# A graph layer whose source rows GpSimd gathers: SyncE also fetches one unit in 72 row by row, and rows, own rows and sets of edges are asked for sooner

## The chip, the cores and the metric

The kernel runs on one core of a Trainium2 chip. The metric is the device time of one execution in microseconds (us); three runs of the kernel before took 15,397.0, 15,399.93 and 15,401.84 us, so the median is 15,399.93 us. A profile of one further execution is read beside it. Engines are named as the profile does: PE is TensorE, DVE is VectorE, ACT is ScalarE, POOL is GpSimd, SP is SyncE (SPq and ACTq are their queues of transfers).

## What is computed

One layer of an equivariant graph network with 50,000 nodes of 160 numbers and 1,650,000 edges, sorted by target. Each edge takes the row of its source node, multiplies it with its own four numbers and with small weight matrices, and the results are summed at the target node; then come a second matrix, a residual and a normalisation.

```
ss, vv = (s[src], v[src])                      # 1,650,000 rows of 160 floats, by index
...
m = jnp.concatenate([out0, out1.reshape(-1, 3 * MUL1)], axis=1)
m_agg = jax.ops.segment_sum(m, dst, num_segments=n)
...
return x + jax.nn.relu(h)                      # h: m_agg times Ws and Wv
...
x = _layernorm(x + _L0_gnn_ref(x, edge_attr_4, ...), axis=-1)
```

The last 50,000 edges of the input are loops of a node to itself; sorted in, each node has one. The kernel takes such an edge out of the list that it gathers for, except at the start, and adds the node's own row in another way.

## The kernel before

**Units, tiles, sets.** 128 edges are a *unit*: one gather, one matmul. Six units (`G`) are a group, three groups (`PG`) a *tile*: 18 units; the program calls a tile a pair. There are 12,516 units in 696 tiles. Seven tiles, 126 units, are a *set of edges* (`SG` = 21 groups); there are 100. The weights are folded into one matrix that is applied after the sums, so per unit only the sums remain: the 128 gathered rows (`xg`, 128 × 160) are multiplied with a 128 × 128 operand `ha`, which holds for each edge its four numbers at the column of its target within a window of 32 nodes.

**The engines' parts.** GpSimd gathers: for each unit an indirect transfer (L433) takes 128 rows of `x` by the offsets in `sources`, into one of four tiles `xg`. VectorE lays out each set (`place`, L358 on: offsets for the gathers at L315, relative targets `rel`, the edges' numbers `pk`), builds `ha` for a tile (`spread`: L442, L445) `AHEAD` = 3 tiles ahead, and turns a tile's sums out of PSUM and adds them to a ring of nodes in SBUF (`turn_sums`: L488, L497). TensorE multiplies (L474), and for finished nodes applies the weights (`block`, L812). The order of SyncE, TensorE, VectorE and ScalarE is the order in which the program is written; GpSimd is arranged by the framework.

**Units that ScalarE fetches.** Every 2.5 tiles from tile 21 on, one unit (the last of its tile) is not gathered. `ask_alone` (L402) reads its 128 addresses from a tile `where` into ScalarE's registers, 32 at a time (L416), and issues 128 plain transfers of one row of 640 bytes each (L421), three after each gather of the loop, from `LEAD` = 4 tiles ahead. They land in one of three tiles `alone_scalar`. TensorE waits for a semaphore that all 128 transfers of the unit raise before it multiplies them. `address` (L394) makes `where` from a set's sources.

**What SyncE does.** All other transfers, in the order of the program: a set's edges (`load`, L259: `raw`, and `fd` with the first target of each group), asked at the first tile of the set before; the nodes' rows for the residual (`xt`, L741) and the results (`out`, L906), in blocks of four times 128 nodes, so about every seven tiles; and the nodes' own rows (`xr`, `sa`: L773, L776), asked five tiles before their part of the ring begins. The write of `out` waits until VectorE has normalised the rows.

**Packs.** The loops are taken out by packing: 128 rows of 790 edges are read (L571 to L575), VectorE finds the loops, moves the later edges up by masked copies (L600 to L663), and SyncE writes each row to its place in the list `edges`, and the loops' numbers to `selves` (`store`, `put`: L698, L715). A pack is a list of 57 steps, the last 17 of which store, 8 rows and 16 transfers each; there are 16 packs. The steps are spread evenly over the time up to the pack's due tile (L973), by which the first set that reads those edges, or the first own rows, need it.

```
for step in packs[0][done:todo]:
    if step:
        step()
```

**How long cover lasts.** `xg` has four tiles, so GpSimd may run three tiles beyond the one that TensorE works on; `sums` of three tiles fit in PSUM.

Of the kernel before, what the change touches and what calls it, by code (L numbers as in the profile page):

```python
# [39 lines left out]
F32 = mybir.dt.float32  # L40
# [10 lines left out]
P = 128  # L51
# [16 lines left out]
PG = 3  # L68
# [9 lines left out]
KM = 31  # L78
AHEAD = 3
SUMS = 3  # L80

ALONE = {"scalar": (2.5, 0, 3)}
LEAD = 4
SEMS = 16
AT_ONCE = 32

# [25 lines left out]
def tile_gnn_resnorm(ctx: ExitStack, tc: tile.TileContext, x, src, dst, attr, W1, W2, W3, W4, W5, Ws, Wv, out, n_edges):  # L112
# [120 lines left out]
    with tc.tile_pool(name="once", bufs=1) as once, tc.tile_pool(name="raw", bufs=2) as rawp, \  # L233
# [7 lines left out]

        wherep, alonep = (later_pools.enter_context(tc.tile_pool(name=name, bufs=bufs))
                          for name, bufs in (("where", 2), ("alone", 3)))
        spotp, ownp = (later_pools.enter_context(tc.tile_pool(name=name, bufs=bufs))
# [148 lines left out]

        def address(s, at, fd, ef, af):  # L394

            where = wherep.tile([P, NK, W], I32, name="where")
            clipped = where.bitcast(F32)
            nc.vector.tensor_scalar(clipped, ef[:, 0], 0.0, float(N - 1), op0=ALU.max, op1=ALU.min)
            nc.vector.tensor_scalar(where, clipped, 4.0 * D, None, op0=ALU.mult)
            where_of[s] = where, at[0]  # L400

        def ask_alone(name, p):  # L402
# [5 lines left out]
            eng, kind = {"sync": (nc.sync, ET.SP), "scalar": (nc.scalar, ET.Activation)}[name]  # L408
            to = alonep.tile([P, D], F32, name=f"alone_{name}")
            sem, uses = kept[name][asked[name] % SEMS], asked[name] // SEMS + 1  # L410
# [452 lines left out]
        def after_pair(p, f, *args):  # L863
            later.setdefault(p, []).append((f, args))
# [43 lines left out]
        def do_cast(s):  # L908
            raws[s] = cast(raws[s])
            address(*raws[s])  # L910

# [83 lines left out]

        to_ask = {name: deque(range_of(every, at)) for name, (every, at, _) in ALONE.items()}
        asking = {}
        turning = None
        for p, (s, g, ng) in enumerate(pairs):
            if p % per == 0 and s + 1 < NSC:  # L1000
                end = reach(s + 1)
                assert end <= 0 or rows_stored[0] == NR or end <= row_start(rows_stored[0])[0][0]
                raws[s + 1] = load(s + 1)
                if s + 2 == NSC:
                    after_pair(p + 4, examine_all)
                    after_pair(p + 6, read_flags)
            if p % per == 2 and s + 1 < NSC:
                do_cast(s + 1)
            rows = gather(s, placed[s], (g - s * SG) * G, ng * G, {b: came[p, b][0] for b in (1, 2) if (p, b) in came})
            for j, ps in enumerate(group_sums(p, rows, has.pop(p))):  # L1010
# [200 lines left out]
```

## Time and profile before

| | |
|---|---|
| median of three runs | 15,399.93 us |
| the profiled execution's own time | 15,395.35 us |
| its span in the profile | 15,393.3 us |
| GpSimd busy | 11,614.3 us (75%) |
| TensorE busy | 10,745.6 us (70%) |
| VectorE busy | 6,891.3 us (45%) |
| ScalarE busy (without issuing transfers) | 138.6 us (1%) |
| TensorE's granted clock | 0.576 |
| moved by the transfer engines | 1,347.79 MB, mean 88 GB/s |

Issuing of transfers by SyncE and ScalarE is not counted as busy; for GpSimd's gathers the issuing itself is the instruction, and it is counted. In a row of groups stand the line, the engine, the operation, output and inputs, the count, then the busy time and the mean in ns of one, then the idle time just before them and what ended most of it. In a row of waits stand who waited for whom, the total in us, how many times, and the longest. The idle time of an engine is of no cost where another engine sets the time.

### The profile page before, as it was taken

How to read it: one execution, taken by the hardware profiler on the slowest of the kernel's cores; microseconds unless marked ns; L12 is line 12 of the kernel's file. 1: busy time of each engine (PE TensorE's matmuls, PEld its weight loads, DVE VectorE, ACT ScalarE, POOL GpSimd, SP SyncE). 2: the span in 40 equal slices, each digit the busy share in tenths (PEclk: the TensorE clock that was granted, in tenths of full speed). 3: DMA queues.
4: the chain of work that ended last, by engine and by line, in shares of the span. 5: the costliest groups of instructions: out<-in, count | busy, mean ns of one | idle time of the engine just before them, and what ended most of it. 6: DMA issues, size and time to landing. Idle time of an engine off the chain costs nothing.

```text
span 15393.3 us, 164322 instructions
## 1 busy us (share of the span) xinstructions
PE 10745.6 (70%) x28959; PEld 6884.0 (45%) x28960; DVE 6891.3 (45%) x9468; ACT 138.6 (1%) x172; POOL 11614.3 (75%) x12263
## 2 busy tenths in 40 slices
PE   6767767676667676666766776766767676667666
PEld 3444444444444444444444444444444444444444
DVE  5534535344353544535344453544535435354333
ACT  0000000000000000000000000000000000000000
POOL 7777777777777777777777777777777777777777
PEclk5555555555555555555556555555555555555555
DMA  3333333333333333333333333333333333333332
GB/s 99 81 99 80 86 93 82 97 83 89 90 85 91 86 87 90 86 92 83 96 84 85 95 80 98 80 88 90 84 95 82 90 90 84 92 85 85 84 83 71
DMA packets 778898, 1347.79 MB, mean 88 GB/s; under 512 B 277566, under 2 KB 536537, under 8 KB 761621
## 3 DMA queue, kind: packets, MB, share of 16 engines
q0 software_dynamic: 587952, 1004.22, 27.7%
q1 hardware_dynamic: 120272, 310.14, 7.3%
q10 hardware_dynamic: 69616, 22.89, 0.8%
q14 instruction: 828, 6.77, 0.2%
q8 instruction: 230, 3.77, 0.1%
HBM read 1264.17 MB, written 72.09 MB: 87 GB/s over the span
## 4 chain that ended last, share of the span: by engine, by line
POOL 60%; issue 23%; DMA 12%; PE 4%; DVE 1%; POOLq 0%
POOL xg L433 60%; DMA xg<-in_x,sources 12%; PE ps L474 3%; PE phb L812 0%; DVE ha L445 0%; DVE xt L815 0%; DVE st L817 0%; DVE xr L791 0%; DVE ring L497 0%; DVE prow L663 0%; DVE ring L795 0%; DVE pri L658 0%; DVE sums L488 0%; DVE mv L819 0%; DVE marks L656 0%
## 5 line engine op out<-in xcount | busy, mean ns | idle before, releaser
L433 POOL DMA_INDIRECT xg<-in_x,sources x12249 | 11609.0, 948 | 3753.2 <-issue 3539.1
L474 PE MATMUL ps<-xg,ha 128*128 128x160 f32 x24498 | 9834.9, 513 | 4624.8 <-DMA xg<-in_x,sources 4521.5
L474 PEld LDWEIGHTS ps<-xg,ha 128*128 128x128 f32 x24498 | 5780.7, 293 | 8482.6 <-DMA xg<-in_x,sources 8005.4
L488 DVE STREAM_TRANSPOSE sums<-ps 128x480 f32<-128x480 f32 x696 | 474.3, 681 | 6929.9 <-PE ps L474 6909.2
L445 DVE TENSOR_TENSOR ha<-hot,pk 128x2304 f32<-128x2304 f32 x696 | 1776.0, 2552 | 23.9
L812 PE MATMUL phb<-BWk,ring 128*128 128x160 f32 (+1 forms) x3910 | 1294.8, 421 | 6.0 <-issue 5.2
L812 PEld LDWEIGHTS phb<-BWk,ring 128*128 128x128 f32 (+1 forms) x3910 | 1104.5, 325 | 7.0 <-issue 5.5
L497 DVE TENSOR_TENSOR ring<-ring,sums 128x160 f32 x2086 | 684.6, 328 | 354.2 <-issue 206.8
L815 DVE SCALAR_TENSOR_TENSOR xt<-phb,xt 128x320 f32<-128x320 f32 x196 | 96.0, 490 | 970.7 <-PE phb L812 970.6
L442 DVE TENSOR_TENSOR hot<-bank,rel 128x576 f32<-128x576 f32 x696 | 521.0, 749 | 0.1
L663 DVE COPY_PREDICATED prow<-marks,prow 128x4734 f32<-128x4734 int32 (+6 forms) x80 | 432.7, 5409 | 0.6
L795 DVE STREAM_TRANSPOSE ring<-xr 128x2560 f32<-128x2560 f32 x96 | 429.3, 4472 | 3.3
L663 DVE COPY_PREDICATED pra<-marks,pra 128x3156 f32<-128x3156 int32 (+6 forms) x80 | 294.8, 3684 | 0.0
L791 DVE TENSOR_TENSOR xr<-xr,bank 128x2560 f32<-128x2560 f32 x96 | 270.1, 2814 | 9.4 <-DMA xr<-in_x 6.1
L474 PE MATMUL ps<-alone_scalar,ha 128*128 128x160 f32 x534 | 196.5, 471 | 0.0
L474 PEld LDWEIGHTS ps<-alone_scalar,ha 128*128 128x128 f32 x534 | 160.1, 335 | 0.0
L494 DVE TENSOR_TENSOR ring<-ring 128x199 f32<-128x199 f32 (+20 forms) x485 | 150.1, 375 | 2.3
L894 ACT ACTIVATE rstd<-mv,eps_t 128x4 f32<-128x4 f32 (+1 forms) x99 | 29.4, 297 | 13513.0 <-DVE mv L819 12291.4
L900 DVE TENSOR_SCALAR xt<-xt,mv,rstd 128x160 f32<-128x160 f32 x391 | 123.2, 376 | 3.6
L751 DVE MEMSET ring<- 128x1255 f32 (+2 forms) x97 | 109.8, 1131 | 20.1 <-issue 19.9
L817 DVE BATCH_NORM_STATS2 st<-xt 128x6 f32<-128x160 f32 x391 | 108.1, 318 | 6.7
L377 DVE STREAM_TRANSPOSE pk<-raw 128x512 f32<-128x512 f32 x100 | 104.2, 1042 | 2.5 <-DMA raw<-in_attr 2.5
(342 smaller groups left out, 1661.5 us busy)
## 6 DMA issues: line engine op xcount, KB each, us to landing
alone_scalar<-in_x ACTq DMA_DIRECT2D x34176, 0.6 KB
xg<-in_x,sources POOLq DMA_INDIRECT x12249
xr<-in_x SPq DMA_DIRECT2D x380, 320.0 KB
edges<-prow SPq DMA_DIRECT2D x2030, 18.5 KB
raw<-edges SPq DMA_DIRECT2D x97, 384.0 KB
selves<-mine SPq DMA_DIRECT2D x2028, 0.5 KB
xt<-in_x SPq DMA_DIRECT2D x97, 320.0 KB
out<-xt SPq DMA_DIRECT2D x97, 320.0 KB
```

The costliest lines, as they stand in the source:

```text
L433: tc.add_to_no_dep_group(f"gathered{s % 2}", nc.gpsimd.indirect_dma_start(out=xg[:, j, :], out_offset=None, in_=x, in_offset=bass.Indirect ...
L442: nc.vector.tensor_tensor(hot[:, :n], slotsP[:, 0:W].unsqueeze(1).to_broadcast([P, n, W]), rel[:, u:u + n].unsqueeze(2).to_broadcast([P, n ...
L445: nc.vector.tensor_tensor(ha[:, :n], hot[:, :n].unsqueeze(2).to_broadcast([P, n, NK, W]), pk[:, :, u:u + n].rearrange("p k u -> p u k").un ...
L474: mm = nc.tensor.matmul(ps[:, j // G, :], ha[:, j].rearrange("p k w -> p (k w)"), xr, start=j % G == 0, stop=j % G == G - 1)
L488: nc.vector.transpose(at[:, :ng], ps[:, :ng].rearrange("p g (b f) -> p g b f", f=FB))
L494: nc.vector.tensor_tensor(ring[k][:, b, :past], ring[k][:, b, :past], ring[k - 1][:, b, S:S + past], op=ALU.add)
L497: nc.vector.tensor_tensor(here, here, at[:, i], op=ALU.add)
L663: nc.vector.copy_predicated(what[:n, a:e], mi[:, r].unsqueeze(2).to_broadcast([n, e - a, what.shape[2]]), what[:n, a + d:e + d])
L791: nc.vector.tensor_tensor(xr[:, :nq], xr[:, :nq], sumP[:, :nq].unsqueeze(2).to_broadcast([P, nq, D]), op=ALU.mult)
L795: nc.vector.transpose(ring[k][:, :, c0:c0 + nq * W].rearrange("p b (w q) -> p q b w", q=nq), xr[:, :nq].rearrange("p q (b f) -> p q b f", ...
L812: wrote("misc", nc.tensor.matmul(ph[:nb, h - h0], nodes, BWk[:, i, :], start=i == 0, stop=i == ND - 1))
L900: nc.vector.tensor_scalar(xt[:n, h], xt[:n, h], mv[:n, h, 0:1], rstd[:n, h:h + 1], op0=ALU.subtract, op1=ALU.mult)
```

## The change

SyncE gets its own list of units: one every four tiles (one in 72) from tile 22 on, fetched like ScalarE's, into two tiles `alone_sync`. Where both engines fetch a unit of one tile, SyncE's is the last and ScalarE's the one before. Rows are no longer issued in fixed numbers after each gather, but by a share that adds up (1.03 × 128 rows over the 72 or 45 gathers from one unit to the next), and from six tiles ahead in place of four.

Because the rows are asked for sooner, so are other things. A set's edges are loaded ten tiles ahead of their set in place of seven (`EARLY`), `address` no longer goes with the cast of a set but stands at the second tile of the set before, own rows are asked seven tiles ahead in place of five (`OWN`), and a pack's due tile is sooner by two or three tiles. `ha` is built two tiles ahead in place of three, so it has three buffers in place of four. The lists of both engines end 12 tiles ahead of the last tile in place of 8.

In the changed kernel the lines of the part shown stand two lower at first (L433 is L435, L474 is L476), later one or two.

```
-AHEAD = 3
+AHEAD = 2
...
-ALONE = {"scalar": (2.5, 0, 3)}
-LEAD = 4
+ALONE = {"sync": (4.0, 1, 2), "scalar": (2.5, 0, 3)}
+LEAD = 6
+OWN = 7
 SEMS = 16
+EARLY = 4
...
-        def address(s, at, fd, ef, af):
+        def address(s, at, ef):
...
-            to = alonep.tile([P, D], F32, name=f"alone_{name}")
+            to = alonep[name].tile([P, D], F32, name=f"alone_{name}")
...
         def do_cast(s):
             raws[s] = cast(raws[s])
-            address(*raws[s])
...
-            due.append(min((first - 1) * per - 1, first_of[own] // PG - 5))
+            due.append(min((first - 2) * per + EARLY - 1, first_of[own] // PG - OWN))
...
-                after_pair(p - 5, ask_own, k, bs, got)
+                after_pair(p - OWN, ask_own, k, bs, got)
...
-        asking = {}
+        asking, share = {}, {name: 0.0 for name in ALONE}
...
-            if p % per == 0 and s + 1 < NSC:
-                end = reach(s + 1)
+            early = 1 if p == 0 else s + 2 if p % per == EARLY else NSC
+            if early < NSC:
+                end = reach(early)
                 assert end <= 0 or rows_stored[0] == NR or end <= row_start(rows_stored[0])[0][0]
-                raws[s + 1] = load(s + 1)
...
+                raws[early] = load(early)
+            if p % per == 1 and s + 1 < NSC and (s + 1) * SG >= NH:
+                address(*[raws[s + 1][i] for i in (0, 1, 5)])
...
                     if name not in asking and of and of[0] - LEAD <= p:
                         asking[name] = ask_alone(name, of.popleft())
-                    for _ in range(ALONE[name][2]):
-                        if name in asking and next(asking[name], 0) == 0:
+                    if name in asking:
+                        share[name] += 1.03 * P / (ALONE[name][0] * PG * G)
+                    while name in asking and share[name] >= 1:
+                        share[name] -= 1
+                        if next(asking[name], 0) == 0:
                             del asking[name]
```

More of the change, by code (lines that the diff above doesn't have):

```diff
@@ L240, in tile_gnn_resnorm @@
             tc.tile_pool(name="psM", bufs=1, space=PSUM) as psM, ExitStack() as later_pools:
-        wherep, alonep = (later_pools.enter_context(tc.tile_pool(name=name, bufs=bufs))
-                          for name, bufs in (("where", 2), ("alone", 3)))
+        wherep = later_pools.enter_context(tc.tile_pool(name="where", bufs=2))
+        alonep = {name: later_pools.enter_context(tc.tile_pool(name=f"alone_{name}", bufs=ALONE[name][2])) for name in ALONE}
         spotp, ownp = (later_pools.enter_context(tc.tile_pool(name=name, bufs=bufs))
@@ L996, in tile_gnn_resnorm @@
         to_ask = {name: deque(range_of(every, at)) for name, (every, at, _) in ALONE.items()}
-        asking = {}
+        asking, share = {}, {name: 0.0 for name in ALONE}
         turning = None
         for p, (s, g, ng) in enumerate(pairs):
-            if p % per == 0 and s + 1 < NSC:
-                end = reach(s + 1)
+            early = 1 if p == 0 else s + 2 if p % per == EARLY else NSC
+            if early < NSC:
+                end = reach(early)
                 assert end <= 0 or rows_stored[0] == NR or end <= row_start(rows_stored[0])[0][0]
-                raws[s + 1] = load(s + 1)
-                if s + 2 == NSC:
-                    after_pair(p + 4, examine_all)
-                    after_pair(p + 6, read_flags)
+                raws[early] = load(early)
+            if p % per == 1 and s + 1 < NSC and (s + 1) * SG >= NH:
+                address(*[raws[s + 1][i] for i in (0, 1, 5)])
+            if p % per == 0 and s + 2 == NSC:
+                after_pair(p + 4, examine_all)
+                after_pair(p + 6, read_flags)
             if p % per == 2 and s + 1 < NSC:
```

## The prediction

> **What bounds the kernel now.** I read the profile's page first (busy time, the chain that ended last, the groups), then the waits of GpSimd, TensorE and VectorE, then GpSimd's work by stretches of time.
>
> ```profile
> span 15393.3 us, 164322 instructions
> PE 10745.6 (70%) x28959; PEld 6884.0 (45%) x28960; DVE 6891.3 (45%) x9468; ACT 138.6 (1%) x172; POOL 11614.3 (75%) x12263
> ...
> POOL 60%; issue 23%; DMA 12%; PE 4%; DVE 1%; POOLq 0%
> ...
> L433 POOL DMA_INDIRECT xg<-in_x,sources x12249 | 11609.0, 948 | 3753.2 <-issue 3539.1
> ```
>
> No engine reaches 80% busy, and still one sets the time. GpSimd makes 12,249 gathers; each occupies it for 948 ns and is followed by a gap. 11,609.0 + 3,753.2 = 15,362.2 us is nearly the whole span, so a gather costs 15,362.2 / 12,249 = 1.2542 us. The next rows say what the gaps are, and who waits for whom.
>
> ```profile
> POOL xg L433 <- issue: 3539.1, 11606, 0.4
> POOL xg L433 <- PE ps L474: 154.9, 508, 0.3
> POOL xg L433 <- DMA xg<-in_x,sources: 50.8, 108, 1.8
> ...
> PE ps L474 <- DMA xg<-in_x,sources: 4521.5, 8641, 5.1
> ...
> PE ps L474 <- DVE ha L445: 14.7, 1, 14.7
> ...
> DVE sums L488 <- PE ps L474: 6909.2, 668, 24.4
> ```
>
> 94% of the gap is "issue": GpSimd waits for nobody. The longest wait put down to TensorE is 0.3 us, no longer than the usual gap, so the ring of four gathered tiles never held it up. TensorE waits for the gather just issued (8,641 times), and VectorE waits for TensorE before 668 of its 696 transposes. Everything trails GpSimd.
>
> ```profile
> 0.00:512.00 512.00, 381.91 (x403) 0.58 0.38 96
> 512.00:1024.00 512.00, 387.24 (x409) 0.56 0.36 87
> 14848.00:15360.00 512.00, 387.33 (x410) 0.58 0.32 77
> ```
>
> In these rows stand GpSimd's busy time and gathers in 512 us. The rate is the same at both ends of the run. ScalarE fetches rows only for tile 21 on, so most of the first stretch has none of that, and it has no more gathers than the others (it loses a few to the start-up). Row fetches on another queue have not slowed the gathers.
>
> **The change part by part.** *Gathers removed.* The built program has 12,084 gathers (12,249 − 165): SyncE takes 166 units and ScalarE one fewer, 266, because the list of asked tiles ends four tiles earlier. 165 × 1.2542 = 206.9 us. By the undisturbed rate of the last stretch, 512/410 = 1.249 us, it would be 206.0; I keep 206.9, since the rare long gaps are part of every stretch.
>
> *What a unit costs SyncE.* No SyncE row fetch is in the trace, but ScalarE's is the same line of code.
>
> ```profile
> alone_scalar<-in_x ACTq DMA_DIRECT2D x34176, 0.6 KB
> ...
> 5003.28 40.42 ACTq L421 DMA_DIRECT2D alone_scalar<-in_x  x101
> ...
> L474 PE MATMUL ps<-alone_scalar,ha 128*128 128x160 f32 x534 | 196.5, 471 | 0.0
> ```
>
> 101 rows in 40.42 us, register loads included, are 0.40 us each, 51.2 us for 128. TensorE idled 0.0 us ahead of these units: they were always there in time. 166 units are 8,500 us of SyncE, and there is room on average:
>
> ```profile
> SPq L906 <- DVE xt L900: 9020.1, 95, 127.7
> SPq L773 <- DVE bank L790: 1748.5, 60, 47.8
> ...
> 4702.19 0.37 SPq L906 DMA_DIRECT2D out<-xt  x1
> 4702.61 0.43 SPq L741 DMA_DIRECT2D xt<-in_x  x1
> 4705.09 0.29 SPq L715 DMA_DIRECT2D edges<-prow  x1
> ...
> 4739.10 0.23 SPq L715 DMA_DIRECT2D selves<-mine  x1
> ...
> L715 SPq DMA_DIRECT2D edges<-prow x2157: 217/227/986, 219.0 to 14286.9; - x197
> L715 SPq DMA_DIRECT2D selves<-mine x2155: 217/227/1094, 219.4 to 14287.3; - x196
> ```
>
> SyncE stands 9,020 + 1,749 us before two lines, waiting for VectorE. That leaves some 4,600 us of its own; with 8,500 it would be used for 86% of 15,190 us. The average hides the tight place, the storing of a pack. 64 stores lie between the two L715 times, 34.2 us, so 0.535 us each. A pack has 4,312/16 = 270 stores, 144 us. They are 17 of a pack's 57 steps, and a pack lasts 696/16 = 43.5 tiles, so they come in 13 tiles. A tile after the change is 12,084/696 × 1.2542 = 21.8 us; 13 tiles are 283 us.
>
> Here is SyncE in the second pack's storing, at the program's fifth write of `out`; before:
>
> ```order
> L715 DMA edges<-prow 1x18960
> L715 DMA selves<-mine 1x512
> L906 DMA out<-xt 128x640
> L741 DMA xt<-in_x 128x640
> L698 TENSOR_LOAD spots
> L715 DMA edges<-prow 1x18960
> L715 DMA selves<-mine 1x512
> ```
>
> and now, at the same write:
>
> ```order
> L423 DMA alone_sync<-in_x 1x640 x6
> L418 TENSOR_LOAD where
> L423 DMA alone_sync<-in_x 1x640 x3
> L908 DMA out<-xt 128x640
> L743 DMA xt<-in_x 128x640
> L423 DMA alone_sync<-in_x 1x640 x16
> L700 TENSOR_LOAD spots
> L717 DMA edges<-prow 1x18960
> L717 DMA selves<-mine 1x512
> ```
>
> Rows now stand on both sides of the write of `out`, which waits for VectorE: while it waits, the rows behind it wait too, and TensorE waits for those. In the 13 tiles SyncE has 144 us of stores, 13 × 12.8 = 166 us of rows (51.2 us in 4 tiles) and about 18 us of other transfers (some 17 at half a microsecond, and waits between them): 328 us in 283. It falls 45 us behind, and regains it in the other 30 tiles, where 12.8 of 21.8 us are used.
>
> *Who feels 45 us.* A unit is dealt at 1.03 × 128/72 = 1.83 rows a gather, so over 128/(18 × 1.83) = 3.9 tiles, from six tiles ahead; its last row is asked 2.1 tiles ahead, and it is the last unit of its tile, another 0.9. That is 3.0 tiles, 65 us, less a landing:
>
> ```profile
> 9011.56 2.60 DMA xg<-in_x,sources
> ...
> 5027.61 1.41 PE L474 MATMUL ps<-xg,ha 128*128 128x160 f32 x4
> ```
>
> With 2.6 us, a gather's landing, 62 us are left: TensorE's new wait for a unit's semaphore should be over when it comes. If it is not, the rest of the tile's matmuls and VectorE's turn stand behind it, but GpSimd has a second cover, the gathered tiles: it may run three tiles, about 60 us, past TensorE. TensorE would catch up, since a unit takes 0.70 us back to back (four passes in 1.41 us) against 1.21 us of GpSimd per unit now. So I cost the fetching at nothing, and it stays at nothing up to a lag of about 62 + 60 = 122 us.
>
> *Moved steps.* Edge sets are loaded three tiles sooner and own rows two; both give more room to what needs them, which the lag above partly uses up. One-hot operands (`ha`) are built two tiles ahead in place of three. VectorE sat waiting for TensorE before 668 turns, so in all but 28 tiles nearly the whole two tiles, 43 us, stay in hand. The two operations on a set's addresses only change places. ScalarE asks two tiles sooner with the same three buffers, 7.5 tiles in all, so it still finds one free. The exception is the start, where the first pack must now be done two tiles sooner and its steps crowd VectorE. VectorE around the second edge set's layout (L315, later L317, writes the offsets for gathers from tile 7 on), before:
>
> ```order
> L341 TENSOR_SCALAR spot<-to 1x18
> L374 STREAM_TRANSPOSE bank<-rf 128x2x4x32
> L377 STREAM_TRANSPOSE pk<-raw 128x4x4x32
> L315 TENSOR_SCALAR sources_137<-bank 128x126
> L383 SCALAR_TENSOR_TENSOR rel<-bank,baseB 128x126
> L387 TENSOR_REDUCE extremes<-rel 128x1
> L388 TENSOR_REDUCE extremes<-rel 128x1
> L600 TENSOR_TENSOR hit<-marks,prow 128x790
> ```
>
> and now:
>
> ```order
> L343 TENSOR_SCALAR spot<-to 1x18
> L376 STREAM_TRANSPOSE bank<-rf 128x2x4x32
> L379 STREAM_TRANSPOSE pk<-raw 128x4x4x32
> L317 TENSOR_SCALAR sources_140<-bank 128x126
> L385 SCALAR_TENSOR_TENSOR rel<-bank,baseB 128x126
> L389 TENSOR_REDUCE extremes<-rel 128x1
> L390 TENSOR_REDUCE extremes<-rel 128x1
> L665 COPY_PREDICATED pra<-marks,pra 128x3128
> ```
>
> Before, the layout stood ahead of the pack's first step; now it stands behind counting, marking and three and a half shifts.
>
> ```profile
> 91.62 0.25 DVE L315 TENSOR_SCALAR sources<-bank 128x126 int32<-128x126 f32 x1
> 92.90 1.56 DVE L600 TENSOR_TENSOR hit<-marks,prow 128x790 f32<-128x790 f32 x1 [0.33 <-ACT marks L599]
> 113.14 0.67 DVE L488 STREAM_TRANSPOSE sums<-ps 128x480 f32<-128x480 f32 x1
> 116.96 3.73 DVE L663 COPY_PREDICATED pra<-marks,pra 128x3156 f32<-128x3156 int32 x1
> 127.92 3.69 DVE L663 COPY_PREDICATED pra<-marks,pra 128x3152 f32<-128x3152 int32 x1
> ...
> L433 POOL DMA_INDIRECT xg<-in_x,sources x12249: 940/946/4374, 6.1 to 15367.1; - x198
> ```
>
> Counting up to the first copy takes 20 us, a copy 3.7, the four operations ahead of one 4: about 20 + 3 × 3.7 + 3 × 4 = 43 us, and 12 us of two turns and two `ha` between. The offsets come 55 us after 92.90, about 148 us. GpSimd needs them after 126 gathers, at 6.1 + 126 × 1.254 = 164 us: 16 us to spare. TensorE waited once for `ha` there, 14.7 us; with a tile less of lead it may be 15 + 22 = 37 us late, inside the 60 us. I allow 2 us here.
>
> *Sum.* The profiled execution took 15,395.35 us (span 15,393.3 and 2.05 around it): 15,395.35 − 206.9 + 2 = 15,190.5. The median of the runs before is 4.6 us above that execution: 15,195.
>
> **The rivals.** *SyncE's rows come too late.* If stores among rows cost more, GpSimd stops when the lag passes 122 us, and each pack then costs the excess. 77 us more over 270 stores is 0.29 each: nothing is lost up to 0.82 us a store, and at 0.82 + 207/(16 × 270) = 0.87 us the gain is gone. At 1.0 us, 16 packs lose 47 us each, 750 us: 15,940, slower. The longest stores in the L715 rows, 0.986 and 1.094 us, speak for it; the medians of 0.227 us and the room after each pack against. I give it 0.11: 0.06 slower, 0.02 near no change, 0.03 a smaller gain.
>
> *The early pile-up reaches GpSimd.* VectorE has no time in hand there:
>
> ```profile
> 112.00:168.00 56.00, 39.47 (x91) 22.34 (x90) 52.95 (x38) 0.00 (x0) 42.29 (x46) 0.50 0.28 66
> 168.00:224.00 56.00, 31.99 (x72) 17.96 (x72) 54.52 (x33) 0.00 (x0) 42.35 (x45) 0.50 0.28 68
> ```
>
> Its busy time is the third figure pair, 53 and 55 of 56 us. If it is 45 us later than worked out, GpSimd loses about 30 us once: 15,225, still faster. 0.06.
>
> *The gathers slow down.* With 12,084 gathers the old time returns at 1.2542 × 12,249/12,084 = 1.2713 us, 17 ns more each. The stretches above speak against any drift. 0.03, half of it slower.
>
> *The transfers are what is shared.* If the 16 transfer engines were the limit, moving the issuing would change nothing: 15,400.
>
> ```profile
> q0 software_dynamic: 587952, 1004.22, 27.7%
> q1 hardware_dynamic: 120272, 310.14, 7.3%
> q10 hardware_dynamic: 69616, 22.89, 0.8%
> ```
>
> They are busy 27.7 + 7.3 + 0.8 = 36% of the time, and 34,176 row fetches take 0.8% (q10), so 21,248 more are worth 0.5%. 0.02. The Trainium skill says this as a rule (DMA: Bandwidth & Descriptors, "Issuing engines are not separate DMA queues"): all queues run on the same 16 engines, and issuing on several at once saves only the sequencer's time to start a transfer, usually small. By that rule the change would be worth little; but what GpSimd spends here, by the L433 row, is just that time, so the trace says that it is not small in this kernel.
>
> **How the numbers follow.** A run of this kernel can be told from no change at about 0.2%, 31 us. The forecast, 15,195, has 0.78. Its ends: 15,180, should part of GpSimd's 50.8 us of gaps put down to a landing go too, and 15,260, which takes in the early pile-up and two or three packs that stall GpSimd by 15 us. Faster: 0.78 + 0.06 + 0.03 + 0.01 = 0.88; same 0.05; slower 0.07.
>
> **What would show it.** Right: 12,084 gathers at 1.25 us, "issue" still GpSimd's wait, no wait of GpSimd over a few microseconds, SyncE's waits for VectorE down by most of 8,500 us, TensorE idle near 0 ahead of `alone_sync`. Wrong: GpSimd waiting tens of microseconds for TensorE during storing (every 43 tiles), or at 160 us for L317, or a gather's pitch above 1.26 us.

## The result, and the profile after

The changed kernel takes 15,488.65 us (median; 15,480.56 to 15,496.85), the kernel before beside it 15,399.93 us (15,397.0 to 15,401.84): a ratio of 1.0058, 95% interval 1.0043 to 1.0073. It is 0.6% slower; 15,195 us was forecast. The profiled execution took 15,496.62 us, 2 us more than its span.

Its page, in the lines that answer to those shown of before:

```profile
span 15494.9 us, 207361 instructions
...
PE 10542.9 (68%) x28959; PEld 6935.5 (45%) x28960; DVE 6886.4 (44%) x9464; ACT 138.6 (1%) x172; POOL 11460.2 (74%) x12098
...
q0 software_dynamic: 580032, 990.69, 28.5%
q1 hardware_dynamic: 162768, 323.82, 7.5%
q10 hardware_dynamic: 69360, 22.81, 0.9%
...
L435 POOL DMA_INDIRECT xg<-in_x,sources x12084 | 11454.9, 948 | 4002.6 <-issue 3412.7
...
L476 PE MATMUL ps<-alone_scalar,ha 128*128 128x160 f32 x532 | 192.5, 464 | 0.0
...
L476 PE MATMUL ps<-alone_sync,ha 128*128 128x160 f32 x332 | 119.3, 461 | 0.0
```

The 165 gathers are gone, a gather still occupies GpSimd for 948 ns, and TensorE idles 0.0 us ahead of both kinds of fetched units. But the gaps grew, from 3,753.2 us ahead of 12,249 gathers to 4,002.6 ahead of 12,084. A gather's pitch is (11,454.9 + 4,002.6) / 12,084 = 1.2792 us in place of 1.2542: 25 ns more, 302 us in all, against 207 saved. The waits say who makes the gaps (who waited for whom, us in all, times, the longest):

```profile
DVE sums L490 <- PE ps L476: 6853.1, 639, 24.9
PE ps L476 <- DMA xg<-in_x,sources: 4726.2, 7253, 6.5
POOL xg L435 <- issue: 3412.7, 11115, 2.1
...
POOL xg L435 <- DMA xg<-in_x,sources: 501.4, 699, 3.3
...
POOL xg L435 <- PE ps L476: 81.7, 252, 3.4
```

GpSimd now waits 501.4 us for its own earlier gathers to land, 699 times; before it was 50.8 us, 108 times. An ordinary gap is 0.305 us (the median of all, in both traces), so beyond it these waits hold 501.4 − 699 × 0.305 = 288 us, and before 18. The difference, 270 us, is most of the 302. It happens in a place that the prediction had taken for recovery. Here are GpSimd's gathers (in brackets) while SyncE stores a pack and after it (the last store comes before 2,156 us):

```profile
2024.00:2090.00 66.00, 49.53 (x53) 0.61 0.39 92
2090.00:2156.00 66.00, 49.82 (x54) 0.50 0.33 77
2156.00:2222.00 66.00, 46.95 (x50) 0.60 0.53 135
2222.00:2288.00 66.00, 42.11 (x45) 0.53 0.31 69
2288.00:2354.00 66.00, 46.97 (x51) 0.61 0.40 91
2354.00:2420.00 66.00, 50.14 (x53) 0.67 0.33 79
```

While SyncE stores, GpSimd keeps its rate, 53 to 54 in 66 us. Afterwards SyncE works off what it owes, 133 and 154 rows in the third and fourth stretch against 71 and 83 in the first two, beside ScalarE's 140 to 160, and GpSimd loses nine gathers in the fourth. This pack is no exception. By the single gathers of the trace, the time by which GpSimd's gaps exceed 0.325 us is 305 us in all. Over the 16 packs, 4 us of it lie while SyncE stores, 186 in the first 132 us after a pack's last store, and 57 in the next 132. The timeline of GpSimd there has the idle time ahead of each gather in its bracket:

```profile
2243.68 0.95 POOL L435 DMA_INDIRECT xg<-in_x,sources  x1 [0.30 <-issue]
2244.93 0.94 POOL L435 DMA_INDIRECT xg<-in_x,sources  x1 [0.30 <-issue]
2246.72 0.94 POOL L435 DMA_INDIRECT xg<-in_x,sources  x1 [0.84 <-DMA xg<-in_x,sources]
2248.82 0.94 POOL L435 DMA_INDIRECT xg<-in_x,sources  x1 [1.16 <-DMA xg<-in_x,sources]
2250.66 0.94 POOL L435 DMA_INDIRECT xg<-in_x,sources  x1 [0.90 <-DMA xg<-in_x,sources]
```

Why a gather waits for another is in the order of the built program, which I had not read with its waits. Four of GpSimd's gathers in a row:

```
L435 DMA xg<-in_x,sources_140 128x160 [waits DMASW6_49]
L435 DMA xg<-in_x,sources_140 128x160 [waits DMASW7_49]
L435 DMA xg<-in_x,sources_140 128x160 [waits DMASW0_49]
L435 DMA xg<-in_x,sources_140 128x160 [waits DMASW1_49]
```

The framework gives the gathers eight semaphores in turn, and a gather waits until the one eight ahead of it, which used the same semaphore, has landed. In the traces of both kernels every gather from the ninth on raises the semaphore that the gather eight ahead of it raised. Eight pitches are 10.0 us: a gather that lands later than that stops GpSimd. The trace of the changed kernel bears this out. A gather's landing can be taken there from the raises of its semaphore, the last before the next gather that uses it. Ahead of the 979 gathers whose eighth predecessor landed 10 us or more after its issue lie 290 us of gap time beyond the ordinary gap; ahead of the 10,202 whose eighth predecessor landed within 9 us lie 9 us.

So the theory (Theory 1): the one-row transfers of two engines at once delay the gathers' landings, and the window of eight turns the delay into GpSimd's time. Against it stood Theory 2, that the moved steps (edge sets, own rows, `ha` two tiles ahead) cost the time, and Theory 3, that any row that SyncE fetches slows the gathers, with or without ScalarE's.

### The profile page after: what moved, and what is told of

Same layout as the page of the kernel before. It is cut to its first block, busy times and chain, and to the rows that moved or that the text cites. A ratio compares the mean times of both kernels' runs of the same rounds, so it can differ in the third digit from the quotient of the medians.

```text
span 15494.9 us, 207361 instructions
## 1 busy us (share of the span) xinstructions
PE 10542.9 (68%) x28959; PEld 6935.5 (45%) x28960; DVE 6886.4 (44%) x9464; ACT 138.6 (1%) x172; POOL 11460.2 (74%) x12098
## 3 DMA queue, kind: packets, MB, share of 16 engines
q1 hardware_dynamic: 162768, 323.82, 7.5%
## 5 line engine op out<-in xcount | busy, mean ns | idle before, releaser
L435 POOL DMA_INDIRECT xg<-in_x,sources x12084 | 11454.9, 948 | 4002.6 <-issue 3412.7
L476 PE MATMUL ps<-xg,ha 128*128 128x160 f32 x24168 | 9581.8, 511 | 4929.2 <-DMA xg<-in_x,sources 4726.2
L476 PEld LDWEIGHTS ps<-xg,ha 128*128 128x128 f32 x24168 | 5783.4, 296 | 8533.2 <-DMA xg<-in_x,sources 7997.7
L476 PE MATMUL ps<-alone_scalar,ha 128*128 128x160 f32 x532 | 192.5, 464 | 0.0
L476 PEld LDWEIGHTS ps<-alone_scalar,ha 128*128 128x128 f32 x532 | 156.2, 328 | 0.0
L476 PE MATMUL ps<-alone_sync,ha 128*128 128x160 f32 x332 | 119.3, 461 | 0.0
```

The costliest lines, as they stand in the source:

```text
L435: tc.add_to_no_dep_group(f"gathered{s % 2}", nc.gpsimd.indirect_dma_start(out=xg[:, j, :], out_offset=None, in_=x, in_offset=bass.Indirect ...
L476: mm = nc.tensor.matmul(ps[:, j // G, :], ha[:, j].rearrange("p k w -> p (k w)"), xr, start=j % G == 0, stop=j % G == G - 1)
```

## Experiments: which part costs

The first four ran on one chip; the kernel before took 15,413.32 us there (15,404.46 to 15,417.05).

**The moved steps alone.** SyncE fetches nothing; all that was moved stays.

```
-ALONE = {"sync": (4.0, 1, 2), "scalar": (2.5, 0, 3)}
+ALONE = {"scalar": (2.5, 0, 3)}
```

> The changed kernel without SyncE's units; everything that was moved stays moved. 266 units are ScalarE's, so 12,250 gathers. Theory 1 (slow landings: rows fetched by transfers of one row all go through one transfer engine; when both queues issue them together its backlog holds up the gathers' shares, and GpSimd does not issue a gather before the eighth one ahead of it has landed): the old pitch, 1.254 us, 15,400 us. Theory 2 (the moved steps are the cost: the pack's crowded start, operands two tiles ahead, sets loaded sooner): the pitch stays near 1.279 us, 15,400 + 300 = 15,700 us. Theory 3 (a SyncE row slows the gathers by itself, wherever it falls, 1.8 us a unit): as theory 1.

Measured: 15,400.43 us (15,387.7 to 15,403.68), ratio 0.9992 (0.9983 to 1.0002).

```profile
L435 POOL DMA_INDIRECT xg<-in_x,sources x12250 | 11610.0, 948 | 3744.3 <-issue 3554.6
```

The pitch is (11,610.0 + 3,744.3) / 12,250 = 1.2534 us, as before. Theory 2 falls: without SyncE's rows the moved steps cost nothing.

**SyncE's rows alone.** ScalarE fetches nothing; its units are gathered again. (Below, the group of gathers and GpSimd's wait for landings.)

```
-ALONE = {"sync": (4.0, 1, 2), "scalar": (2.5, 0, 3)}
+ALONE = {"sync": (4.0, 1, 2)}
```

> The changed kernel without ScalarE's units; SyncE's 166 stay. 12,350 gathers. Theory 1: one queue of rows is what the kernel before had, so the pitch stays near 1.254 us: 15,400 + 101 x 1.254 = 15,527 us, up to 15,560. Theory 3: 300 us more, about 15,830 us.

Measured: 15,551.97 us, ratio 1.0091 (1.0074 to 1.0107).

```profile
L435 POOL DMA_INDIRECT xg<-in_x,sources x12350 | 11703.2, 948 | 3808.4 <-issue 3569.0
```

```profile
POOL xg L435 <- DMA xg<-in_x,sources: 79.5, 127, 2.2
```

12,350 gathers are 101 more than before, worth 126.7 us: 15,540. SyncE's rows cost the other 12 us; the pitch is 1.2560. The same rows that cost 302 us beside ScalarE's cost nearly nothing alone, so Theory 3 falls.

**Half as many for SyncE.** A unit every eight tiles, dealt at the same pace, so that SyncE fetches half of the time.

```
-ALONE = {"sync": (4.0, 1, 2), "scalar": (2.5, 0, 3)}
+ALONE = {"sync": (8.0, 1, 2), "scalar": (2.5, 0, 3)}
...
-                        share[name] += 1.03 * P / (ALONE[name][0] * PG * G)
+                        share[name] += 1.03 * P / (min(ALONE[name][0], 4.0) * PG * G)
```

> SyncE takes one unit in eight tiles, 83, each dealt at the same pace as in the changed kernel, with four tiles of rest. 12,167 gathers, worth 103 us against the kernel before. Theory 1: the backlog drains in the rests and SyncE has none left over from storing, so the cost falls by much more than half, under 100 us: 15,300 to 15,400 us. Theory 3: half the cost, 150 us: 15,447 us.

Measured: 15,379.52 us (15,367.5 to 15,384.55), ratio 0.9978 (0.9968 to 0.9987): 0.2% less than before.

```profile
L435 POOL DMA_INDIRECT xg<-in_x,sources x12167 | 11532.3, 948 | 3799.0 <-issue 3515.4
```

```profile
POOL xg L435 <- DMA xg<-in_x,sources: 167.0, 294, 2.4
```

82 gathers fewer should have made 15,310; 69 us of it are lost (pitch 1.2601). Half the rows bring about a quarter of the loss. This fits the window: a landing costs nothing until it comes some ten microseconds after the issue, so the loss grows faster than the rows.

**Without the window of eight.** The changed kernel, but each gather raises a semaphore of its own out of 72 (the units of four tiles), and TensorE waits for that before the unit's matmuls. Nothing else is changed.

```
+LANES = 4 * PG * 6
...
+                i = (p % 4 * PG * G + j) % LANES
+                lane_uses[i] += 1
+                d.then_inc(lanes[i], 16)
+                tc.no_tile_sem_insts.add(d.ins.name)
...
+                landed[p, j] = lanes[i], 16 * lane_uses[i], f"unit{p}_{j}"
...
+                if (p, j) in landed:
+                    alone = None, *landed.pop((p, j))
```

> The changed kernel, with a semaphore for each of the 72 places of a gathered unit in place of eight in turn, so that GpSimd no longer waits for the gather eight ahead to have landed; TensorE waits for each unit as before. Theory 1: gathers land late as before, but GpSimd does not feel it; the pitch is 1.251 us or a little less than before, 15,175 to 15,200 us. If GpSimd's slow stretches have another cause (its own queue being full, a contended memory), the pitch stays near 1.279 us and the time near 15,490 us.

Measured: **15,194.34 us** (15,192.57 to 15,194.97), ratio 0.9858 (0.9841 to 0.9874) to the kernel before. That is less than both kernels take (the changed one was timed on another chip, beside 15,399.93 us). Its group of gathers, and GpSimd's and TensorE's waits (TensorE's wait for a gather is now one of its sequencer, "PEq"):

```profile
L439 POOL DMA_INDIRECT xg<-in_x,sources x12084 | 11468.8, 949 | 3688.4 <-issue 3551.5
...
L489 PE MATMUL ps<-alone_sync,ha 128*128 128x160 f32 x332 | 118.0, 457 | 5.8 <-PEq L488 5.8
```

```profile
PE ps L489 <- PEq L488: 4516.8, 6963, 7.0
...
POOL xg L439 <- issue: 3551.5, 11636, 0.3
...
POOL xg L439 <- PE ps L489: 73.5, 241, 0.3
...
POOL xg L439 <- PEq L488: 57.1, 187, 0.3
```

None of these waits of GpSimd exceeds 0.3 us, the ordinary gap, and the pitch is (11,468.8 + 3,688.4) / 12,084 = 1.2543 us: the 165 gathers are worth what they were forecast to be worth. The landings themselves are as late as ever. From the issue of a gather to the start of its unit's first matmul pass (its landing, or TensorE if that is later), taken from the trace's single instructions:

| kernel | median, us | 99 of 100 under, us | over 10 us |
|---|---|---|---|
| before | 2.70 | 9.1 | 72 |
| changed | 6.30 | 12.8 | 1,114 |
| SyncE's rows alone | 2.69 | 11.3 | 160 |
| half as many for SyncE | 4.77 | 11.4 | 336 |
| changed, 72 semaphores | 6.70 | 13.4 | 1,789 |

In the changed kernel's worst stretch, 2,222 to 2,288 us, the mean is 11.4 us, over the window. With 72 semaphores even more gathers are late, since GpSimd no longer pauses for them. Only TensorE waits for them, and with four tiles `xg` GpSimd does not feel that: its waits for TensorE are ordinary gaps.

## Experiments: why gathers land late

The trace's records of single packets (queue, size, start, duration) show what a one-row transfer meets. From the issue of a ScalarE row to its packet's start it takes 1.04 us before (median) and 3.59 us after. The issuing itself has not slowed: successive rows of ScalarE are 0.318 us apart in both traces (median), SyncE's 0.322. And packets of the two queues avoid each other: SyncE's row packets take up 7.8% of the time, but only 0.15% of ScalarE's row packets start more than 10 ns before the end of one, while 21% start inside a row packet of a gather. So both engines' one-row transfers seem to pass through one transfer engine, one at a time. The Trainium skill says so (DMA: Bandwidth & Descriptors, "Why a DMA increments its semaphore by 16 and not by 1"): a transfer issued by SyncE or ScalarE is split over as many engines, up to 16, as divide its slowest dimension, on the lowest-numbered ones, so a single row gets one, while a gather counts as landed only when all 16 have reported. The trace agrees as far as it goes, for it does not name engines: with each single row goes one packet of 4 bytes (34,256 of them on ScalarE's queue q10 for 34,048 rows), and a gather's semaphore is raised sixteen times (10,508 of the changed kernel's 12,084 gathers have all sixteen on record).

The sixteen raises also tell which part of a gather is late. Medians, from the gathers with all sixteen on record:

| kernel | issue to 15th raise, us | issue to 16th, us |
|---|---|---|
| before | 2.57 | 2.64 |
| changed | 2.60 | 6.13 |
| SyncE's rows alone | 2.55 | 2.62 |
| changed, 72 semaphores | 2.58 | 6.42 |

In the changed kernel the first fifteen come as soon as ever, and the last is 3.5 us late. One report of sixteen is held up, and not the gather as a whole. That fits a queue at one place, which the rows and a sixteenth of each gather share.

Three explanations were put to the test. 1a: the rows' bytes fill that one engine. 1b: the bytes and packets beside the gathers matter, wherever they run. 1c: the number of transfers, or of their issues, matters. Two kernels change only how SyncE's unit is cut; in both, the rows after the first of a transfer are the next ones in memory and not those that the edges name.

**16 rows a transfer.** Eight transfers a unit in place of 128, by the quoted rule over 16 engines.

```
+            R = 16 if name == "sync" else 1
...
+                        if k % R == 0:
+                            d = eng.dma_start(to[e:e + R, :].bitcast(U8), xbytes[ds(v[k], R * 4 * D)].rearrange("(o f) -> o f", o=R))
```

> The changed kernel, but SyncE fetches each of its units in 8 transfers of 16 consecutive rows each in place of 128 transfers of one row (the rows after the first are not those the edges name, so sums of these units are not the reference's; the bytes are the same). Theory 1a (one-row transfers of all queues stand one behind another at one of the 16 transfer engines, and a gather that needs that engine for its last bytes lands late): 16 rows spread over 16 engines, so gathers are not delayed: pitch 1.254 to 1.257 us, 15,195 to 15,215 us. Rival 1b (what delays the gathers is the sheer bytes and packets beside them, wherever they run): pitch still near 1.279 us, about 15,490 us. Rival 1c (it is the number of transfers or SyncE's issuing): 8 in place of 128 gives the same low time as 1a, and the kernel with 17 rows each tells them apart. On a chip on which ScalarE's issuing is slow itself (the kernel before near 24,800 us) none of this can be told.

**17 rows a transfer.** Seven transfers of 17 rows and one of 9; by the same rule 17 rows get one engine.

```
+                        R = min(17, P - e) if name == "sync" else 1
+                        if name != "sync" or e % 17 == 0:
```

> As the kernel with 16 rows each, but 7 transfers of 17 consecutive rows and one of 9 for each of SyncE's units (again not the reference's rows in these units). On a chip where issuing was slow, 17 rows came 28 ns one after another, as one-row transfers do, and 16 rows came in parallel. Theory 1a (one engine): 17 rows at one engine take 17 times 28 ns, about 0.5 us, at once, so gathers are delayed as by one-row transfers or somewhat less: pitch 1.262 to 1.28 us, 15,290 to 15,490 us. Rival 1c (the number of transfers or the issuing): as with 16 rows, 15,195 to 15,215 us.

Measured, beside 15,404.41 us for the kernel before: 15,205.73 us with 16 (ratio 0.9871, 0.9854 to 0.9887), 15,204.47 us with 17 (0.987, 0.9854 to 0.9887). The profiled execution with 16 was its longest, 15,245.09 us, with a pitch of 1.2584 us and 951 ns a gather. From the page and from GpSimd's waits, first with 16 rows, then with 17:

```profile
q1 hardware_dynamic: 162768, 323.82, 7.7%
...
L437 POOL DMA_INDIRECT xg<-in_x,sources x12084 | 11492.8, 951 | 3713.6 <-issue 3495.3
```

```profile
POOL xg L437 <- DMA xg<-in_x,sources: 63.8, 128, 2.5
```

```profile
q1 hardware_dynamic: 144176, 323.75, 7.6%
...
L437 POOL DMA_INDIRECT xg<-in_x,sources x12084 | 11455.5, 948 | 3711.8 <-issue 3493.5
```

```profile
POOL xg L437 <- DMA xg<-in_x,sources: 69.5, 140, 2.5
```

With 16 rows the queue q1 moves as many packets and bytes as in the changed kernel, 162,768 and 323.82 MB, and the loss is gone: 1b falls. With 17 it is gone too (pitch 1.2551 us), though these rows do seem to pass one by one through the engine of ScalarE's rows: some 0.4% of ScalarE's row packets start inside one, against some 3% with 16 rows (SyncE's row packets take up 5.7% and 6.3% of the time). The packets agree: with 17 rows q1 has 162,768 − 144,176 = 18,592 fewer, 112 for each of the 166 units, all of 4 bytes. That is 16 a unit in place of 128: one for each transfer of 17 rows and nine for that of 9. So 1a falls as I had put it, with the bytes as what counts, and I had expected 15,290 to 15,490 there. Issue to matmul is back at 2.67 and 2.74 us, the 16th raise at 2.58 and 2.60 us, the delay of a ScalarE row at 1.01 and 1.05 us. What counts is the number of transfers, 1c, at the one place that delays a gather's last report; the two kernels do not tell the transfers from their issues and their packets of 4 bytes, which become fewer there with them. Why a row takes as long as it does there is only partly seen: in the changed kernel, with 10 to 20 rows waiting, row packets start some 0.22 us apart in the mean but 0.035 us apart in the median, in bursts, while the two engines together, when both issue, ask for one every 0.16 us. A queue that is asked faster than it is served fits the delay. What holds it between bursts, no run shows.

## Experiments where rows were issued slowly

Twelve more runs fell into sessions in which the kernel before itself takes 24,500 to 24,900 us. Two of these sessions carry the chip number 12, and so does the session of 16 and 17 rows above, with 15,404.41 us: the slowness is not shown to belong to a chip. The bound is another one there. Of the kernel before with 72 semaphores, the chain that ended last and TensorE's longest waits:

```profile
ACTq 51%; issue 29%; PE 1%; DVE 1%; DMA 1%; PEld 0%; ACT 0%; PEldq 0%; SPq 0%; DVEq 0%
```

```profile
PE ps L487 <- PEq L486: 12496.6, 233, 100.3
POOL xg L437 <- PE ps L487: 5809.8, 238, 78.5
```

ScalarE's rows come too late, TensorE waits for them up to 100 us, and GpSimd for TensorE. Two timeline rows of ScalarE, the changed kernel in its ordinary run and the kernel before with 72 semaphores in a slow session:

```profile
2245.44 16.61 ACTq L423 DMA_DIRECT2D alone_scalar<-in_x  x41
```

```profile
2196.98 47.64 ACTq L422 DMA_DIRECT2D alone_scalar<-in_x  x40
```

40 rows take 47.6 us in place of 16.6 for 41. The times of these runs cannot test the theory, and they are given in short.

**72 semaphores in the kernel before** (the edit above without SyncE's rows), run three times.

> The kernel before (no SyncE units, 12,249 gathers) with a semaphore for each of the 72 places of a gathered unit. Theory 1: its landings were in time already, so there is little to gain: only part of the 51 us that GpSimd waited for landings, 15,380 to 15,415 us beside about 15,410 for the kernel before. If the semaphores made the gathers cheaper by themselves (a shorter wait on each, whatever lands late), the gain of 300 us that they brought with SyncE's units shows here too: 15,110 us.

> The kernel before, with a semaphore of its own for each of 72 gathers in turn in place of eight shared ones; no rows by SyncE; the same kernel as in the run where ScalarE's issuing was slow, on another chip. Theory 1 (a gather may not be issued before the gather eight ahead of it has landed, and only the rows of two engines together make landings that late): before, GpSimd's waits for a landing are 50.8 us in all, so at most these go: 15,380 to 15,415 us. Rival (own semaphores make any gather cheaper, and the 1.4% of the changed kernel with them comes from that and not from SyncE's units): some 200 us less here too, about 15,210 us, with a pitch near 1.238 us.

> The kernel before, with a semaphore of its own for each of 72 gathers in turn in place of eight shared ones; no rows by SyncE. Theory 1 (a gather may not be issued before the gather eight ahead of it has landed, and only the one-row transfers of two engines together make landings that late): before, GpSimd's waits for a landing are 50.8 us in all, so at most these go: 15,350 to 15,415 us. Rival (own semaphores make any gather cheaper, and the 1.4% of the changed kernel with them comes from that and not from SyncE's units): some 200 us less here too, about 15,210 us, with a pitch near 1.238 us.

Measured 24,935.79, 24,887.69 and 24,628.17 us beside 24,812.77, 24,791.17 and 24,504.07; ratios 1.0049 (1.0021 to 1.0076), 1.0042 (1.0026 to 1.0059), 1.0046 (1.0028 to 1.0065): 0.4 to 0.5% slower each time, and what costs that is not shown. Inconclusive for the theory. The rival, that own semaphores make every gather cheaper, has its answer in the traces: with them the median gap ahead of a gather is 0.305 us in these three runs, as it is with eight in the kernel before, and in the changed kernel the pitch with them is 1.2543 us, as before the change without them.

**More units for SyncE, with 72 semaphores:** one every 3, then every 3.5 tiles, with three buffers.

```
-ALONE = {"sync": (4.0, 1, 2), "scalar": (2.5, 0, 3)}
+ALONE = {"sync": (3.5, 1, 3), "scalar": (2.5, 0, 3)}
```

> The changed kernel with a semaphore for each place, and one SyncE unit every three tiles in place of four, three tiles alone_sync: 221 units, 55 gathers fewer, worth 69 us if GpSimd still sets the time: 15,125 us. SyncE is then asked for 17.1 us of rows a tile, so in 13 tiles of storing 222 + 144 + 18 = 384 us in 283: 100 us behind, over the 62 us that rows are asked ahead. If that reaches GpSimd through TensorE, the gain is eaten: 15,200 us or more.

> The changed kernel with own semaphores for the gathers, and SyncE's unit every 3.5 tiles in place of 4, with three buffers in place of two: some 24 gathers fewer. Theory 1 (without the eight-landing window each gather taken from GpSimd is worth its 1.254 us as long as SyncE keeps up): 24 x 1.254 = 30 us less than with every 4 tiles, about 15,165 us. Rival (SyncE is now the bound while it stores a pack: 54 us a unit in 3.5 tiles leave it 60 to 80 us behind there, and TensorE waits for its rows): 15,190 us or more, with TensorE's waits for SyncE's queue over 200 us.

> The changed kernel with own semaphores for the gathers, and SyncE's unit every 3.5 tiles in place of 4, with three buffers in place of two: 24 gathers fewer. Theory 1 (without the eight-landing window each gather taken from GpSimd is worth its 1.254 us as long as SyncE keeps up): 24 x 1.254 = 30 us less than with every 4 tiles, about 15,165 us. Rival (SyncE is now the bound while it stores a pack: some 50 us a unit in 3.5 tiles leave it 60 to 80 us behind there, and TensorE waits for its rows): 15,190 us or more, with TensorE's waits for SyncE's rows over 100 us.

Every 3: 26,246.77 us beside 24,812.77, ratio 1.0577 (1.055 to 1.0603). Every 3.5: 26,111.06 beside 24,791.17 (1.0534, 1.0516 to 1.0551), and again 25,950.89 beside 24,504.07 (1.0586, 1.0566 to 1.0607). Whether more units pay where rows are issued at the ordinary speed stays open.

**16 and 17 rows a transfer**, the edits above, run three times each. With 16 rows:

> The changed kernel with its eight semaphores, but SyncE fetches each unit in 8 transfers of 16 rows that stand together in x, starting at the row of the first edge of each 16 (so these units' sums are not the reference's); same bytes, same 128 rows, an eighth of a percent of the issues. Theory 1a (one row per transfer goes through one transfer engine, and that engine's backlog is the trouble): 16 rows spread over 16 engines, no backlog; pitch 1.254 us, 15,195 to 15,215 us. Theory 1b (the bytes or rows on SyncE's queue hold up the gathers wherever they go): near 15,490 us.

> The changed kernel, but SyncE fetches each of its units in 8 transfers of 16 consecutive rows each in place of 128 transfers of one row (the rows after the first are not those the edges name, so sums of these units are not the reference's; the bytes are the same). Theory 1a (one-row transfers of all queues stand one behind another at one of the 16 transfer engines, and a gather that needs that engine for its last bytes lands late): 16 rows spread over 16 engines, so gathers are not delayed: pitch 1.254 to 1.257 us, 15,195 to 15,215 us. Rival 1b (what delays the gathers is the sheer bytes and packets beside them, wherever they run): pitch still near 1.279 us, about 15,490 us. Rival 1c (it is the number of transfers or SyncE's issuing): 8 in place of 128 gives the same low time as 1a, and the next kernel, with 17 rows each, tells them apart.

> The changed kernel, but SyncE fetches each of its units in 8 transfers of 16 consecutive rows each in place of 128 transfers of one row (the rows after the first are not those the edges name, so sums of these units are not the reference's; the bytes are the same). Theory 1a (one-row transfers of all queues stand one behind another at one of the 16 transfer engines, and a gather that needs that engine for its last bytes lands late): 16 rows spread over 16 engines, so gathers are not delayed: pitch 1.254 to 1.257 us, 15,195 to 15,215 us. Rival 1b (what delays the gathers is the sheer bytes and packets beside them, wherever they run): pitch still near 1.279 us, about 15,490 us. Rival 1c (it is the number of transfers or SyncE's issuing): 8 in place of 128 gives the same low time as 1a, and the kernel with 17 rows each tells them apart. On the chips on which ScalarE's issuing is slow itself (the kernel before near 24,800 us) none of this can be told.

With 17 rows:

> As the run with 16 rows, but 7 transfers of 17 rows and one of 9 (these units' sums are not the reference's either). 17 is a prime over 16, so if a transfer is split over as many of the 16 engines as divide its rows, as the Trainium skill says (DMA: Bandwidth & Descriptors, why a DMA increments its semaphore by 16), all 17 rows go through one engine. Theory 1a: the one engine has its 119 of 128 rows again, so the gathers slow down: 15,300 to 15,490 us, clearly above the run with 16 rows. Theory 1c (the number of transfers, 128 a unit, is the trouble, not where they go): as the run with 16 rows, 15,195 to 15,215 us.

> As the kernel with 16 rows each, but 7 transfers of 17 consecutive rows and one of 9 for each of SyncE's units (again not the reference's rows in these units). In the earlier run 17 rows came 28 ns one after another, as one-row transfers do, and 16 rows came in parallel. Theory 1a (one engine): 17 rows at one engine take 17 times 28 ns, about 0.5 us, at once, so gathers are delayed as by one-row transfers or somewhat less: pitch 1.262 to 1.28 us, 15,290 to 15,490 us. Rival 1c (the number of transfers or the issuing): as with 16 rows, 15,195 to 15,215 us.

> As the kernel with 16 rows each, but 7 transfers of 17 consecutive rows and one of 9 for each of SyncE's units (again not the reference's rows in these units). On a chip where issuing was slow, 17 rows came 28 ns one after another, as one-row transfers do, and 16 rows came in parallel. Theory 1a (one engine): 17 rows at one engine take 17 times 28 ns, about 0.5 us, at once, so gathers are delayed as by one-row transfers or somewhat less: pitch 1.262 to 1.28 us, 15,290 to 15,490 us. Rival 1c (the number of transfers or the issuing): as with 16 rows, 15,195 to 15,215 us.

Measured: 16 rows 25,776.89, 25,740.29 and 25,861.89 us, 17 rows 25,831.3, 25,734.8 and 25,860.17, beside 24,812.77, 24,791.17 and 24,892.02; ratios 1.038 to 1.040, the intervals within 1.036 and 1.0431. Taking gathers off GpSimd brought nothing where GpSimd waits for TensorE and TensorE for issued rows; which part of the change makes these kernels slower there, no run shows.

## Why the prediction was wrong, point by point

- *Gathers removed, 165 × 1.2542 = 206.9 us*: right. The count is 12,084, and with 72 semaphores the kernel takes 15,194.34 us against 15,195 forecast; with 16 rows a transfer 15,206. Beside the kernel before, timed with them, these are 219 and 199 us less, where 205 was forecast; that one of them meets the forecast time to a microsecond is luck.
- *SyncE fetches at no cost as far as SyncE and TensorE go*: right. Units are there in time (0.0 us idle ahead of them), and of SyncE's 9,020.1 us of waiting at the write of `out`, 927.5 are left (the first line is new: SyncE waits for TensorE before it may fill a tile `alone_sync` again):

```profile
SPq L423 <- PEq L475: 1221.3, 72, 39.3
SPq L908 <- DVE xt L902: 927.5, 37, 99.0
SPq L717 <- DMA edges<-prow: 695.7, 658, 5.0
```

- *Moved steps, 2 us*: right within the measurement, by the first experiment (0.9992, interval 0.9983 to 1.0002).
- *"Row fetches on another queue have not slowed the gathers"*: the step that failed. The rows that it rested on compare no fetching queue with one; from one to two is another step. One queue leaves a landing's median at 2.7 us, whichever engine issues; two at once make it 6.3 us. The sum kept 1.2542 us for each of the 12,084 gathers left; they took 1.2792. The price is 25 ns a gather, and the break-even that the rival "the gathers slow down" worked out was 17 ns. That rival, with 0.03, is what happened.
- *"The transfers are what is shared", 0.02*: I priced SyncE's rows at 0.5% of 16 engines. Of a gather's sixteen raises only the last is late, so what is crowded is one of sixteen, and an average over 16 said nothing about it. Yet the rival as priced (15,400, nothing to gain) was wrong too: the gain is there once landings may be late.
- *The sum* had no term for how late a landing may be before GpSimd feels it. The cover that I counted (three tiles of `xg`, 60 us) is not the one that binds; the eight semaphores are, with 10 us.
- *The wrong sign's mark*, a pitch above 1.26 us, is what the trace shows. Its other mark, stalls of tens of microseconds during storing, is absent: the loss comes after storing, when SyncE's rows are no longer thinned by stores (4 us of 305 lie within the storing). The prediction had SyncE fall 45 us behind there and regain it at no cost; the regaining is where the gathers land too late.
- *"At 1.0 us, 16 packs lose 47 us each"*: by its own figures it is 45 + 270 × 0.465 − 122 = 49. Nothing else rests on it.

The Trainium skill's rule (DMA: Bandwidth & Descriptors, "Issuing engines are not separate DMA queues"), that issuing on several engines saves only the sequencer's usually small time, is half right here: the saving is 1.4% with 72 semaphores, by the ratio 0.9858, and with eight the late landings take back 2.0% (1.0058 / 0.9858).

## What to carry to other kernels

Read the built program's waits, and not only the time they take: a semaphore used in turn is a limit on how many transfers may be in flight, and it costs nothing in a trace until landings reach it. Price many small transfers by their number, and check from packets of the two queues whether they ever overlap; a mean over the transfer engines hides a queue at one of them. If landings are late but early enough for their user, give them semaphores of their own before taking load away.

## What was not expected of the hardware

- Two streams of one-row transfers delay each other and the gathers beside them: a ScalarE row's packet starts 3.59 us after its issue in place of 1.04, a gather's unit is multiplied 6.30 us after its issue in place of 2.70. Only the last of a gather's sixteen raises is late (6.13 us after the issue in place of 2.64; the 15th 2.60 and 2.57). Where SyncE fetches 16 or 17 rows in one transfer, at the same bytes, none of this is seen (1.01 and 1.05 us, 2.67 and 2.74 us).
- Sessions differ by far more than the change: the same kernel before took 15,400 to 15,413 us in some and 24,504 to 24,892 us in others, at a similar granted clock (0.573 to 0.578 and 0.597 to 0.600). One-row issues came about 1.2 us apart over stretches in the slow ones, in place of 0.4; why they did is not known.
